# Moving two GpSimd additions of `bv` behind the block differences of `h` in a fused two-layer graph kernel

## Chip, cores and metric

The kernel runs on one core of one Trainium2 chip. The metric is the device time of one execution in microseconds; the time before is the median of three runs. All arithmetic is in float32.

## What is computed

128 batches, each a 128 x 512 matrix `x` (128 nodes, 512 features). Layer 0 adds to every row a number that depends on the adjacency matrix; layer 1 is multi-head attention with 8 heads of 64, masked where the adjacency is zero:

```python
h = relu(layernorm(x))
A = adj @ h;  C = adj @ h + b
x = x + max over n' of relu(A[o, n] + C[o, n'] - A[o, n'])
h = relu(layernorm(x))
q, k, v = h @ Wq + bq, h @ Wk + bk, h @ Wv + bv
w = softmax(q k^T / 8 + mask(adj))
x = x + w v
```

In layer 0 the two matrices are the same, so `C - A` is the bias `b` alone and the layer adds to a row a number of that row: `relu(max(adj @ h) + b)`. A number per row does not change a layernorm over the row, so one normalisation serves both layers. The weights of a softmax sum to one, so `bv` can be added to `x` directly instead of to `v`. That is what the moved additions do: `x += bv` for a batch, on GpSimd.

## The kernel before

The 128 batches are taken in 32 groups of 4 (`G`, L54; `NG`, L184). The loop over groups (L700) is a software pipeline, in an order that is written out by hand: `tc.manual_schedule()` (L655) leaves each engine the order in which the program issues its instructions. While group g goes through attention, the inputs of the projections of group g+1 are prepared, and the layernorms of group g+2 run. Here `m` (L717) is the first batch of group g+2.

**A group's stages.** First `apply(g-1)` (L584): attention weights times V, 128 TensorE matmuls at L600, and the normalisation on VectorE at L617 and L618. Then `scores(g)` (L563): 64 matmuls at L570, exponentials on ScalarE at L578. Then comes a list of steps (`part`, L705): six for the product h Wv of group g (v), six for h Wq of group g+1 (q), six for h Wk (k). Behind step s the program issues all that `todo[s]` holds (L757 to L761).

**The products.** `Products` (L392) forms each projection by a Strassen-like scheme with 7 products of half size, called p1, p6, p2, p7, p5 and the pair p4 and p3; all their matmuls have line L421 (`mm`). The last two products are in turn split once more into 128 x 128 blocks, in two parts: `p43a` (L492) directly behind p7 and `p43b` (L511) behind p5. Their matmuls have line L487 (`block_mm`). Results come out of PSUM by VectorE additions: L460 in p6, L469 in p7, L442 in p5 and p43b (`add`), and L490 (`more`), which adds a small block from the PSUM bank `scr` (L479) onto `u` in SBUF. `p43a` fills `scr` and ends with three L490 additions out of it. `p43b` first writes into the same `scr`, so its first matmuls on TensorE wait for these three. It then adds from `scr` once more (fourth L490), and its last four matmuls write into `scr` again and wait for that addition.

**The operands.** The scheme needs sums of quarters of h: `h_sum` (L340, instruction at L345), four subtractions of two SBUF tiles into `hs` on VectorE per group, for the next group. They are issued behind steps 0, 1, 2 and 2 of a group (L727), except in group 0. The blocks need differences as well: `h_blocks` (L347, instructions at L359), six subtractions on GpSimd into the single buffer `h2`, issued behind steps 5 and 6 (L729). The old `h2` is read by the matmuls of v's `p43b` until then.

**The layernorms.** `norm(m)` (L264) computes statistics on VectorE (L279 to L282) and from them `rstd` and `nmr` on GpSimd (L284, L286). `norm_end(m)` (L288) computes `hn` on ScalarE (L289) and then calls `add_bv(m)` (L293), a GpSimd addition of two SBUF tiles of 128 x 512, in place in the tile `xp` of x (L295). `blocks(m)` (L297) transposes `hn` in 32 x 32 blocks on VectorE (L302), `move` sends the blocks to their places by DMA, and `adjacency(m)` (L324) is the layer-0 product (L327) and its maximum (L328). `next_norms(m)` (L644) says behind which step each of these is issued for groups 0 to 29: `norm_end` of m and m+1 behind step 0, `norm` and `norm_end` of m+2 behind step 8 and of m+3 behind step 12.

**GpSimd's other work in a group.** Four additions of the residual for the group before (L630), and eight multiplications of the attention weights by the mask (`mask`, L580, instruction at L582) behind steps 8 to 15, which `apply` of the next group needs.

Of the kernel before, what the change touches and what calls it, by code (L numbers as in the profile page):

```python
# [53 lines left out]
G = 4  # L54
# [113 lines left out]
def tile_adj_preln_d2(  # L168
# [38 lines left out]
    def fast(ctx):  # L207
# [15 lines left out]
        def x_of(b):  # L223
            return X[b // 2][:, b % 2, :]
# [60 lines left out]
            nmr = NMR[m] = stat.tile([P, 1], F32, name="nmr")  # L285
            nc.gpsimd.tensor_scalar(nmr, mv[:, 0:1], rstd, -1.0, op0=ALU.mult, op1=ALU.mult)  # L286

        def norm_end(m):  # L288
            nc.scalar.activation(HN[m], x_of(m), AF.Relu, scale=RSTD[m], bias=NMR[m])  # L289
            if m >= G:  # L290
                add_bv(m)

        def add_bv(m):  # L293
            x_m = x_of(m)
            nc.gpsimd.tensor_tensor(x_m, x_m, bv_sb, op=ALU.add)  # L295
# [348 lines left out]
        def next_norms(m):  # L644

            return {
                0: [(norm_end, m), (norm_end, m + 1)],
                4: [(blocks, m)], 6: [(blocks, m + 1), (move, m + 1)], 7: [(adjacency, m)],
                8: [(norm, m + 2), (norm_end, m + 2)],
                12: [(norm, m + 3), (norm_end, m + 3), (adjacency, m + 1)],  # L650
                13: [(blocks, m + 2)],
                14: [(blocks, m + 3), (move, m + 3), (adjacency, m + 2)],
            }

        with tc.manual_schedule():  # L655
# [44 lines left out]
            for g in range(NG):  # L700
# [16 lines left out]
                m = b + 2 * G  # L717
                if g + 1 < NG:
# [12 lines left out]
                    if g + 2 < NG:  # L731
                        for s, l in next_norms(m).items():
                            for what in l:
                                add(s, *what)
                    else:
                        add(6, count, 0, b)
# [73 lines left out]
```

## Time and profile before

| what | value |
|---|---|
| time, median of 3 runs (lowest, highest) | 1538.81 us (1538.68, 1539.62) |
| span of the profiled execution | 1538.4 us |
| VectorE busy | 1080.2 us, 70% |
| GpSimd busy | 869.5 us, 57% |
| ScalarE busy | 507.0 us, 33% |
| granted TensorE clock, mean | 0.998 |
| GpSimd L295, the additions of bv | 128, mean 1464 ns, 186.1 us in all |
| GpSimd L582, the masks | 240, mean 1271 ns, 297.4 us in all |
| DMA | 105.32 MB, mean 68 GB/s |

PE stands for TensorE's matmuls, PEld for its weight loads, DVE for VectorE, ACT for ScalarE, POOL for GpSimd. Durations of an instruction are in ns, everything else is in us. In the timeline, a row gives the start, the time from the first start to the last end of the instructions merged in it (x8 is eight of them), the engine, the line and the operation with its tiles, and in brackets the idle time of the engine just before and what ended it. The ends of matmuls are modelled, so for TensorE the starts are the better measure.

### The profile page before, as it was taken

To read this page: it belongs to the slowest core of one execution; us is meant where nothing else is said; L and a number is where in the kernel's file an instruction comes from. 1 tells how busy PE (TensorE), PEld (TensorE's weight loads), DVE (VectorE), ACT (ScalarE), POOL (GpSimd) and SP (SyncE) were. 2 spreads that over 40 slices of the span, in tenths; PEclk is the share of its full clock that TensorE was granted. 3 is DMA by queue.
4 is the path that set the end of the run, shared out by engine and by line. 5 is a ranking of instruction groups with operands and counts; after the bars stand their busy time and mean duration, and the time that the engine had idled before them with its cause. 6 is when DMAs were issued, how large, how long until landed. Compare 5 with 4: busy or idle time off the path is not lost. (4 is left out here: it accounts for less than half of the span.)

```text
span 1538.4 us, 33066 instructions
## 1 busy us (share of the span) xinstructions
PE 1507.3 (98%) x12909; PEld 1322.5 (86%) x12909; DVE 1080.2 (70%) x2187; ACT 507.0 (33%) x970; POOL 869.5 (57%) x968
## 2 busy tenths in 40 slices
PE   8999999999999999999999999999999999999997
PEld 6888888888888888888888888888888888888886
DVE  6677677776777767677767777677676767776766
ACT  3333323333243332333332333324333233333232
POOL 5676556556565564655655655656556465565620
PEclk9999999999999999999999999999999999999999
DMA  5222222223222232222322222322223222232211
GB/s 169 52 68 79 60 62 73 64 75 78 47 73 66 72 83 43 75 65 73 79 56 65 74 64 76 72 52 73 65 72 84 42 75 68 70 80 56 51 33 57
DMA packets 307807, 105.32 MB, mean 68 GB/s; under 512 B 273153, under 2 KB 273281, under 8 KB 307649
## 3 DMA queue, kind: packets, MB, share of 16 engines
q1 hardware_dynamic: 307328, 102.84, 26.0%
q8 instruction: 104, 1.70, 0.5%
q14 instruction: 55, 0.44, 0.1%
q0 software_dynamic: 176, 0.27, 0.1%
q10 hardware_dynamic: 144, 0.07, 0.0%
HBM read 37.03 MB, written 33.55 MB: 46 GB/s over the span
## 5 line engine op out<-in xcount | busy, mean ns | idle before, releaser
L630 POOL TENSOR_TENSOR o<-xp,o 128x512 f32<-128x512 f32 x122 | 151.0, 1270 | 312.6 <-DVE o L618 269.3
L582 POOL TENSOR_TENSOR w<-w,live 128x512 f32<-128x512 f32 x240 | 297.4, 1271 | 0.0
L490 DVE TENSOR_TENSOR u<-u,bk 128x256 f32<-128x256 f32 x552 | 206.0, 415 | 120.3 <-PE bk L487 113.1
L578 ACT ACTIVATE w<-bk 128x512 f32<-128x512 f32 x256 | 128.8, 628 | 345.4 <-PE bk L570 345.4
L295 POOL TENSOR_TENSOR xp<-xp,bv_sb 128x512 f32<-128x512 f32 x128 | 186.1, 1464 | 61.0 <-ACT hn L289 61.0
L421 PEld LDWEIGHTS bk<-hs,sk_sb 128*128 128x128 f32 x768 | 143.7, 190 | 44.5 <-issue 29.2
L421 PE MATMUL bk<-hs,sk_sb 128*128 128x256 f32 x768 | 181.4, 379 | 0.0
L421 PE MATMUL bk<-sv_sb,hs 128*128 128x256 f32 x768 | 181.2, 379 | 0.0
L421 PE MATMUL bk<-hs,sq_sb 128*128 128x256 f32 x744 | 175.9, 379 | 0.0
L421 PEld LDWEIGHTS bk<-sv_sb,hs 128*128 128x128 f32 x768 | 143.8, 190 | 30.9 <-issue 14.3
L328 DVE TENSOR_REDUCE amax<-bk 128x1 f32<-128x512 f32 x128 | 88.2, 689 | 108.0 <-PE bk L327 105.1
L421 PEld LDWEIGHTS bk<-hs,sq_sb 128*128 128x128 f32 x744 | 139.1, 190 | 17.5
L284 POOL TENSOR_TENSOR rstd<-ve,mhalf 128x1 f32<-128x1 f32 x128 | 83.5, 653 | 95.1 <-DVE ve L282 94.9
L289 ACT ACTIVATE hn<-xp,nmr,rstd 128x512 f32<-128x512 f32 x124 | 100.8, 814 | 104.7 <-POOL nmr L286 104.7
L469 DVE TENSOR_TENSOR u<-bk,u 128x512 f32<-128x512 f32 x95 | 65.3, 688 | 91.8 <-PE bk L421 89.7
L327 PE MATMUL bk<-hn,adjT 128*128 128x512 f32 x248 | 126.7, 592 | 0.0
L600 PE MATMUL bk<-v,w 128*64 128x65 f32 x4096 | 126.6, 222 | 0.0
L600 PEld LDWEIGHTS bk<-v,w 128*64 128x64 f32 x4096 | 122.1, 137 | 4.1 <-issue 0.3
L421 PE MATMUL bk<-wv_sb,hT 128*128 128x256 f32 x512 | 124.3, 386 | 0.0
L570 PE MATMUL bk<-qT,kT 64*128 64x128 f32 x2048 | 122.9, 275 | 0.0
L421 PE MATMUL bk<-hT,wk_sb 128*128 128x256 f32 x512 | 121.1, 380 | 0.0
L570 PEld LDWEIGHTS bk<-qT,kT 64*128 64x128 f32 x2048 | 116.8, 188 | 2.5 <-issue 0.3
(149 smaller groups left out, 2576.6 us busy)
## 6 DMA issues: line engine op xcount, KB each, us to landing
out_dram<-o SPq DMA_DIRECT2D x128, 256.0 KB, 2.0
xp<-in_x_dram SPq DMA_DIRECT2D x62, 512.0 KB, 3.8
hT<-tb SPq DMA_DIRECT2D x992, 32.0 KB, 1.9
xp<-in_x_dram SPq DMA_DIRECT2D x4, 256.0 KB, 4.1
wq_sb<-in_L_gnn_Wq_dram SPq DMA_DIRECT2D x2, 512.0 KB, 7.7
wk_sb<-in_L_gnn_Wk_dram SPq DMA_DIRECT2D x2, 512.0 KB, 9.7
wv_sb<-in_L_gnn_Wv_dram SPq DMA_DIRECT2D x2, 512.0 KB, 10.3
bv_sb<-in_L_gnn_bv_dram POOLq DMA_DIRECT2D x1, 256.0 KB, 6.8
```

Of the source, the lines that this page charges most:

```text
L284: nc.gpsimd.tensor_tensor(rstd, ve, mhalf, op=ALU.pow)
L289: nc.scalar.activation(HN[m], x_of(m), AF.Relu, scale=RSTD[m], bias=NMR[m])
L295: nc.gpsimd.tensor_tensor(x_m, x_m, bv_sb, op=ALU.add)
L327: nc.tensor.matmul(pa, adjT, HN[m], start=True, stop=True)
L328: nc.vector.reduce_max(AMAX[g][:, i : i + 1], pa, axis=AX.X)
L421: nc.tensor.matmul(bank[:, r, :], lhs, rhs, start=first and r == 0 and c == 0, stop=r == 1 and c == 1, skip_group_check=True,)
L490: nc.vector.tensor_tensor(to, to, what, op=ALU.add)
L570: nc.tensor.matmul(psc[j][:, f, :], KT[g][r, f, i * D : (i + 1) * D], QT[g][r, f, i * D : (i + 1) * D], start=True, stop=True,)
L578: nc.scalar.activation(w[:, j], psc[j], AF.Exp, scale=HD ** -0.5)
L582: eng.tensor_tensor(w[:, j], w[:, j], live_h, op=ALU.mult)
L600: nc.tensor.matmul(pav[r, c : c + HE], w[:, h % 2, h // 2, r], V[:, i, h, :], start=True, stop=True,)
L630: eng.tensor_tensor(y, x_of(b), y, op=ALU.add)
```

## The change

`norm_end` gets an argument, by which `next_norms` leaves out the additions of bv for the first two batches of a group (m and m+1), and issues them behind step 6 instead. There they come behind both `h_blocks` calls (which the loop adds to steps 5 and 6 ahead of `next_norms`). The additions for m+2 and m+3 stay where they are, and so does every instruction of the other engines. It is for GpSimd's order: the additions no longer stand directly behind the `nmr` of m+1, and fill the place behind the block differences.

```diff
-        def norm_end(m):
+        def norm_end(m, bv=True):
             nc.scalar.activation(HN[m], x_of(m), AF.Relu, scale=RSTD[m], bias=NMR[m])
-            if m >= G:
+            if m >= G and bv:
                 add_bv(m)
@@
             return {
-                0: [(norm_end, m), (norm_end, m + 1)],
-                4: [(blocks, m)], 6: [(blocks, m + 1), (move, m + 1)], 7: [(adjacency, m)],
+                0: [(norm_end, m, False), (norm_end, m + 1, False)],
+                4: [(blocks, m)],
+                6: [(blocks, m + 1), (move, m + 1), (add_bv, m), (add_bv, m + 1)], 7: [(adjacency, m)],
                 8: [(norm, m + 2), (norm_end, m + 2)],
```

In GpSimd's queue, a group's instructions before and after:

```
before: 4 x L630, rstd, nmr, rstd, nmr, 2 x L295, 6 x L359,           rstd, nmr (m+2), L295, 5 x L582, ...
after:  4 x L630, rstd, nmr, rstd, nmr,           6 x L359, 2 x L295, rstd, nmr (m+2), L295, 5 x L582, ...
```

## The prediction

> **What bounds the kernel now.** I read the page's busy times first, then the waits, then one group in the timeline, engine by engine.
>
> ```profile
> PE 1507.3 (98%) x12909; PEld 1322.5 (86%) x12909; DVE 1080.2 (70%) x2187; ACT 507.0 (33%) x970; POOL 869.5 (57%) x968
> ```
>
> TensorE is the bound, with 31 us of the span idle, start and end included. A change on GpSimd can only pay through a wait of TensorE. The list of waits (engine, line, waited for, us in total, times, longest) has few of these:
>
> ```profile
> POOL h L359 <- PE bk L487: 155.4, 30, 9.9
> PEld bk L487 <- DVE u L490: 27.2, 29, 1.1
> PE bk L487 <- DVE u L490: 15.6, 29, 0.7
> ```
>
> TensorE never waits for GpSimd. It waits 29 times for VectorE's L490, once per group. And the block differences L359, ahead of which the additions of bv stand, wait for TensorE for 5 us in nearly every group, so a place nearer the front of GpSimd's queue gives them nothing. The question is what makes L490 late. One group (g = 10) in the timeline, rows of GpSimd, VectorE and TensorE in order of time:
>
> ```profile
> 525.99 3.38 POOL L295 TENSOR_TENSOR xp<-xp,bv_sb 128x512 f32<-128x512 f32 x2
> 526.49 1.75 DVE L345 TENSOR_TENSOR hs<-hT 128x512 f32<-128x512 f32 x1
> 528.17 1.75 DVE L345 TENSOR_TENSOR hs<-hT,hs 128x512 f32<-128x512 f32 x1
> 529.34 1.89 PE L421 MATMUL bk<-sv_sb,hs 128*128 128x256 f32 x8
> 529.85 0.68 DVE L469 TENSOR_TENSOR u<-bk,u 128x512 f32<-128x512 f32 x1
> 530.63 1.08 DVE L490 TENSOR_TENSOR u<-u,bk 128x256 f32<-128x256 f32 x3
> 531.77 0.71 PE L487 MATMUL bk<-ssv_sb,h 128*128 128x128 f32 x4 [0.53 <-DVE u L490]
> 534.10 1.89 PE L421 MATMUL bk<-hT,wq_sb 128*128 128x256 f32 x8
> 534.35 0.73 POOL L359 TENSOR_TENSOR h<-hT 128x256 f32<-128x256 f32 x1 [4.97 <-PE bk L487]
> ```
>
> The third and fourth h_sum take 1.75 us and lie under the two additions of bv. L469, the three L490 and then p43b on TensorE follow without a gap. Group 30 runs the same v product, and `next_norms` gives it no additions of bv:
>
> ```profile
> 1473.98 0.68 DVE L345 TENSOR_TENSOR hs<-hT 128x512 f32<-128x512 f32 x1
> 1474.59 0.69 DVE L345 TENSOR_TENSOR hs<-hT,hs 128x512 f32<-128x512 f32 x1
> 1476.16 0.69 DVE L469 TENSOR_TENSOR u<-bk,u 128x512 f32<-128x512 f32 x1 [0.89 <-PE bk L421]
> 1476.85 1.89 PE L421 MATMUL bk<-sv_sb,hs 128*128 128x256 f32 x8
> 1478.58 0.61 PE L487 MATMUL bk<-ssv_sb,h 128*128 128x128 f32 x4
> 1481.01 0.81 PE L421 MATMUL bk<-hT,wq_sb 128*128 128x256 f32 x3
> ```
>
> There the same two h_sums take 0.68 and 0.69 us, VectorE waits 0.89 us for TensorE instead, and p43b starts 1.73 us behind p5 (1478.58 - 1476.85) instead of 2.43 (531.77 - 529.34). This is the comparison that carries the forecast.
>
> [...] L345 (two SBUF inputs) is stretched under L295, from 0.69 to 1.75 us, and of the two L295 the pair takes 3.38 us where two undisturbed ones would take 2.5 (the masks L582 of the same shape: 1.27 us). L460, L469, L442 and L490, with one input in PSUM, have a maximum of 694 ns (L490: 423 ns) over all their executions, many of them under masks. [...]
>
> **The change part by part.**
>
> 1. *Removed from behind the nmr of m+1.* GpSimd is then idle from 526.0 (the end of the second nmr) until L359. The third and fourth h_sum fall from 1.75 to 0.69 us, so VectorE is done with them about 2.1 us earlier: in group 30 the fourth ends 1.05 us behind the start of p7 (1475.28 - 1474.23). L469 then waits for p7's matmuls, as in group 30 and as in q, where it starts 2.0 us behind p7 (542.14 - 540.14); in v of group 10 it is 3.12 (529.85 - 526.73). So L469 and the three L490 come 1.1 to 1.2 us earlier. In group 30 the L490 end at 1478.13, 0.24 us ahead of the weight load of p43b (1478.37): the wait of 0.93 us on the weight load is gone whole.
>
> 2. *What appears in its place.* In p43b the last four matmuls wait for the fourth L490. That queue on VectorE is L442 (p5), then `blocks(m)` L302 of 0.70 us from step 4, then L490. With p43b late, L490 has time; with p43b on time, it does not quite. In q, where nothing stands between L442 and L490, the stretch from p5's first matmul to the next product's first is 546.72 - 542.76 = 3.96 us. In group 30 a mask of 0.68 us stands there (L582 on VectorE at 1479.39), and the stretch is 1481.01 - 1476.85 = 4.16. So of the 4.76 us in group 10 (534.10 - 529.34), 0.80 are lost, and I take 0.60 of them to come back; with 0.70 in place of 0.68 us, 0.58. I take 0.59.
>
> 3. *How many groups.* I followed this stretch through the trace: it is 4.76 to 4.78 us in 27 of the groups 1 to 29, and 4.92 and 4.64 in the two others; 3.96 in q throughout but one at 4.07. Group 0 does not count: its h_sums come behind steps 3 to 5, when its additions (51.62 to 54.11) are over, and they take 0.68 us already. So 29 groups: 29 x 0.59 = 17.1 us.
>
> 4. *Added behind the block differences.* L359 waits for the last read of `h2` by p43b (534.35, GpSimd idle 4.97 us before), and its six take 3.56 us until 537.91. The two additions follow: their cost is between 2.5 us (2 x 1.27, undisturbed) and 3.4 (as now). What is queued behind is rstd of m+2, which waits for VectorE's statistics until 540.46. 537.91 + 2.5 = 540.4: they fit. At 3.4 rstd is 0.9 us late. Who waits for that: nmr, hn(m+2), its addition, five masks, and the last mask ends at 556.95. `apply` begins at 560.29, so 3.3 us are free: nothing reaches TensorE. The hn of m+2 on ScalarE delays the p1a of k at 548.65, ahead of which ScalarE idles 5.81 us. I take 0.
>
> 5. *VectorE under the new place.* It runs L302, L460, L328 and L279 there (536.29 to 539.90): each has one SBUF input at most. L279 keeps 677 to 695 ns in all 128 executions, though some lie under masks. I take 0. In group 0 the differences end at 63.8, so the two additions end at 66.3 to 67.2; the rstd behind them starts at 66.75 now, so it is at most 0.4 us late, ahead of the same slack: 0.
>
> 6. *No new wait.* The additions wait for hn of the same batch, done at 526.9. Nobody reads the new xp until add_c, two groups later.
>
> Sum: 1538.8 - 17.1 = 1521.7 us.
>
> **The rivals.**
>
> *The whole loss comes back* (7%). If L302 and L490 are in time for the last four matmuls: 29 x 0.80 = 23.2, so 1515.6. Against it stands group 30, whose mask is as long as L302.
>
> *Nothing happens* (5%). If the h_sums are slow for a reason of their own, such as the DMA traffic (GpSimd's additions lie in the stretch with 116 to 223 GB/s), they stay at 1.75: 1538.8. For it: in group 30, where they are short, the traffic is lower too (66 GB/s from 1472 to 1476). Against: the L345 at 524.57 lies in the densest traffic of the group (223 GB/s) and takes 0.69.
>
> *The collision moves, and it is slower* (4%). If L460, L328 and L279 were stretched by 1.06 us each under the additions, q's L469 (idle 1.76 us before) would come 3.18 - 1.76 = 1.42 late. In v, 1.12 to 1.19 late cost 0.80, so some 1.1 here: 29 x (1.1 - 0.59) = +15, 1554. Against: the fixed durations of these lines.
>
> **How the numbers follow.** My case has 84%. Its own bounds are 29 x 0.58 = 16.8 and, if part of the 0.2 returns, up to the 23.2 of the first rival; downwards, a wait like the one of L302 might cost 0.2 more: 29 x 0.4 = 11.6, 1527.2. The range is 1515 to 1527; it leaves out the last two rivals. Faster by over 0.2% (3.1 us): 91%; within: 5%; slower: 4%.
>
> **What would show it.** In the profile after: L345 near 690 ns in all groups (now 1191 and 1196 on average); L295 near 1270; the wait of L487's weight load for L490 no longer 0.93 but 0.1 to 0.2 us, in the last four matmuls; the stretch from p5 to q's p1 at 4.16 to 4.18; a group's period 0.6 us shorter. It is wrong if L345 stays long, if L460, L328 or L279 become longer, or if TensorE waits elsewhere for what these 0.6 us uncover.

## The result, and the profile after

The changed kernel takes 1521.37 us (median of 4 runs, 1520.96 to 1521.57); the kernel before takes 1538.85 us beside it. The ratio is 0.9885, with a 95% interval of 0.9868 to 0.9902: faster by 17.5 us. Forecast were 1521.7 us, in a range of 1515 to 1527.

The page's busy times and two rows of the waits (engine, line, waited for, us in total, times, longest), after the change:

```profile
PE 1504.1 (99%) x12909; PEld 1325.6 (87%) x12909; DVE 1023.2 (67%) x2187; ACT 507.3 (33%) x970; POOL 844.4 (56%) x968
POOL h L359 <- PE bk L487: 233.8, 30, 9.9
DVE u L469 <- PE bk L421: 114.6, 94, 2.7
```

VectorE lost 57 us of busy time (1080.2 before) and GpSimd 25 us (869.5), with as many instructions as before. The two waits of TensorE's L487 for L490 are gone from the list. VectorE's L469 now waits for TensorE 94 times instead of 65: in the 29 groups in question the late one has become the early one. The timeline of a group (g = 10, the one shown of before), rows of VectorE, TensorE and GpSimd in order of time:

```profile
519.97 0.68 DVE L345 TENSOR_TENSOR hs<-hT 128x512 f32<-128x512 f32 x1
520.58 0.68 DVE L345 TENSOR_TENSOR hs<-hT,hs 128x512 f32<-128x512 f32 x1
522.13 0.69 DVE L469 TENSOR_TENSOR u<-bk,u 128x512 f32<-128x512 f32 x1 [0.88 <-PE bk L421]
522.82 1.89 PE L421 MATMUL bk<-sv_sb,hs 128*128 128x256 f32 x8
523.02 1.08 DVE L490 TENSOR_TENSOR u<-u,bk 128x256 f32<-128x256 f32 x3 [0.20 <-PE bk L487]
524.55 0.61 PE L487 MATMUL bk<-ssv_sb,h 128*128 128x128 f32 x4
525.36 0.70 DVE L302 STREAM_TRANSPOSE tb<-hn 128x512 f32<-128x512 f32 x1
525.99 0.38 DVE L490 TENSOR_TENSOR u<-u,bk 128x256 f32<-128x256 f32 x1
526.11 0.39 PE L487 MATMUL bk<-sv_sb,h 128*128 128x128 f32 x2
526.42 0.71 PE L487 MATMUL bk<-ssv_sb,h 128*128 128x128 f32 x4
526.97 1.89 PE L421 MATMUL bk<-hT,wq_sb 128*128 128x256 f32 x8
527.22 0.73 POOL L359 TENSOR_TENSOR h<-hT 128x256 f32<-128x256 f32 x1 [7.71 <-PE bk L487]
530.73 2.50 POOL L295 TENSOR_TENSOR xp<-xp,bv_sb 128x512 f32<-128x512 f32 x2
533.33 0.55 POOL L284 TENSOR_TENSOR rstd<-ve,mhalf 128x1 f32<-128x1 f32 x1
```

The two h_sums take 0.68 us instead of 1.75. p43b on TensorE starts 1.73 us behind p5 (524.55 - 522.82), the stretch from p5 to q's first product is 526.97 - 522.82 = 4.15 us, and it is 4.14 or 4.15 in all of the groups 1 to 29. A group's period fell from 47.37 us (529.34 and 576.71 are p5 of groups 10 and 11 before) to 46.75 (522.82 and 569.57). The two additions take 2.50 us in their new place and end at 533.23, and rstd of m+2 starts at 533.33.

From group 1's p5 to group 30's, the trace of before has 1373.85 us (103.00 to 1476.85) and that of after 1355.85 (102.07 to 1457.92): 18.0 us, in 29 groups. The profiled spans differ by 19.2 us; most of the rest comes from ahead of the groups, where TensorE's first large products (L546) started 1.1 us earlier in the profiled execution of the changed kernel (12.15 against 13.29), before any of the changed code. The timed difference, 17.5 us, is close to that of the groups.

### The profile page after: what moved, and what is told of

The parts are those of the page before. It is cut to its first block, busy times and chain, and to the rows that moved or that the text cites. A ratio compares the mean times of both kernels' runs of the same rounds, so it can differ in the third digit from the quotient of the medians.

```text
span 1519.2 us, 33036 instructions
## 1 busy us (share of the span) xinstructions
PE 1504.1 (99%) x12909; PEld 1325.6 (87%) x12909; DVE 1023.2 (67%) x2187; ACT 507.3 (33%) x970; POOL 844.4 (56%) x968
## 4 chain that ended last, share of the span: by engine, by line
PE 99%; DVE 0%; DMA 0%; POOL 0%; ACT 0%; DVEq 0%; issue 0%
PE bk L421 55%; PE bk L487 19%; PE bk L600 8%; PE bk L570 8%; PE bk L327 7%; PE bk L546 1%; PE bk L321 0%; DMA xp<-in_x_dram 0%; DVE o L618 0%; ACT o L289 0%; DVE live L639 0%; DVE st L279 0%; DVE RS L617 0%; DVE o L630 0%; DVEq L776 0%; POOL rstd L284 0%
## 5 line engine op out<-in xcount | busy, mean ns | idle before, releaser
L490 DVE TENSOR_TENSOR u<-u,bk 128x256 f32<-128x256 f32 x552 | 205.7, 414 | 115.4 <-PE bk L487 111.3
L295 POOL TENSOR_TENSOR xp<-xp,bv_sb 128x512 f32<-128x512 f32 x128 | 161.1, 1269 | 59.5 <-ACT hn L289 58.6
L328 DVE TENSOR_REDUCE amax<-bk 128x1 f32<-128x512 f32 x128 | 88.2, 689 | 105.4 <-PE bk L327 102.5
L359 POOL TENSOR_TENSOR h<-hT 128x256 f32<-128x256 f32 x31 | 22.6, 728 | 238.2 <-PE bk L487 233.8
L421 PEld LDWEIGHTS bk<-hs,sq_sb 128*128 128x128 f32 x744 | 138.9, 190 | 17.7
L469 DVE TENSOR_TENSOR u<-bk,u 128x512 f32<-128x512 f32 x95 | 65.8, 692 | 116.7 <-PE bk L421 114.6
```

What stands on the lines that cost most here:

```text
L328: nc.vector.reduce_max(AMAX[g][:, i : i + 1], pa, axis=AX.X)
L421: nc.tensor.matmul(bank[:, r, :], lhs, rhs, start=first and r == 0 and c == 0, stop=r == 1 and c == 1, skip_group_check=True,)
L490: nc.vector.tensor_tensor(to, to, what, op=ALU.add)
```

## Experiments

My theory: a two-input h_sum on VectorE and a GpSimd instruction that reads SBUF lengthen each other (in group 10 before, the h_sum takes 1.75 us instead of 0.69, each addition 1.7 instead of 1.27); the stretched h_sums make L469 and the three L490 late, and TensorE's p43b waits for them; behind that a second, shorter wait stands, on the transpose L302. The rivals: it is the place of `x += bv` in the order that counts, not what it collides with (order); any work of GpSimd slows VectorE (busy); the loss is proportional to the number of additions (proportional); v's product is longer of itself. A further rival, that DMA traffic makes the h_sums slow, is settled by the changed kernel's own trace (see the part on the prediction). All times below are medians beside the kernel before on the same chip, 1539.6 us for the first four and 1539.5 for the last three. In the kernels e1 to e3 the lines behind L296 have numbers 5 higher.

### e1: the additions again in the old place, as dummies

In the three kernels e1 to e3, `extra` stands in the old place of the additions, whose own place remains the new one. Its output is a tile that nobody reads at that time, so this is additional work only.

```diff
+        def extra(m):
+            t = tmp.tile([P, 2, HT2], F32, name="p1a", bufs=1).rearrange("p a b -> p (a b)")
+            for i in range(2):
+                nc.gpsimd.tensor_tensor(t, x_of(m + i), bv_sb, op=ALU.add)
@@
-                0: [(norm_end, m, False), (norm_end, m + 1, False)],
+                0: [(norm_end, m, False), (norm_end, m + 1, False), (extra, m)],
```

> The changed kernel, and in the place which the two additions of bv left (behind the nmr of m+1) two additions of the same operands into a tile that nobody reads; the moved additions stay behind the block differences. Extra work, same output. Collision of reads: the third and fourth h_sum are 1.75 us again, v's stretch from p5 to the next product 4.76 us, the time that of the kernel before, 1538.8 (+-1.5). Rival 'order' (the gain is that x += bv itself comes later, and what depends on it): no effect, 1521.4.

Measured: 1539.58 us, ratio 1.0000 (0.9992 to 1.0009). Its timeline, rows of GpSimd, VectorE and TensorE:

```profile
525.30 3.39 POOL L300 TENSOR_TENSOR p1a<-xp,bv_sb 128x512 f32<-128x512 f32 x2
525.80 1.76 DVE L350 TENSOR_TENSOR hs<-hT 128x512 f32<-128x512 f32 x1
527.48 1.75 DVE L350 TENSOR_TENSOR hs<-hT,hs 128x512 f32<-128x512 f32 x1
528.65 1.89 PE L426 MATMUL bk<-sv_sb,hs 128*128 128x256 f32 x8
533.41 0.81 PE L426 MATMUL bk<-hT,wq_sb 128*128 128x256 f32 x3
```

The whole gain is gone, the h_sums take 1.76 and 1.75 us, and the stretch is 4.76 us again (528.65 to 533.41), though the additions that count stand in their new place. The rival "order" falls: what matters is what runs beside the h_sums.

### e2: GpSimd busy in the old place, reading nothing

```diff
-            for i in range(2):
-                nc.gpsimd.tensor_tensor(t, x_of(m + i), bv_sb, op=ALU.add)
+            for i in range(4):
+                nc.gpsimd.memset(t, 0.0)
```

> The changed kernel, and in the old place four GpSimd memsets of 128x512 into a tile that nobody reads: GpSimd is busy but reads nothing from SBUF. Collision of reads: h_sum stays at 0.69 us, 1521.4 (+-1.5). Rival 'busy' (any work of GpSimd beside h_sum slows it[...]): h_sums stretched as far as the memsets last, up to 1538.8.

Measured: 1521.83 us, ratio 0.9885 (0.9869 to 0.9902), as the changed kernel.

```profile
520.18 2.27 POOL L300 MEMSET p1a<- 128x512 f32 x4
520.70 0.68 DVE L350 TENSOR_TENSOR hs<-hT 128x512 f32<-128x512 f32 x1
521.31 0.68 DVE L350 TENSOR_TENSOR hs<-hT,hs 128x512 f32<-128x512 f32 x1
```

Four memsets fill 2.27 us, and the h_sums under them keep 0.68. The rival "busy" falls: beside the memsets, which only write, an h_sum takes 0.68 us, and beside the additions of e1, which also read, 1.75.

### e3: one input instead of two

```diff
-            for i in range(2):
-                nc.gpsimd.tensor_tensor(t, x_of(m + i), bv_sb, op=ALU.add)
+            for i in range(3):
+                nc.gpsimd.tensor_scalar(t, x_of(m + i % 2), 1.0, 2.0, op0=ALU.mult, op1=ALU.add)
```

> The changed kernel, and in the old place three GpSimd multiply-adds with constants, each reading one SBUF tile of 128x512, into a tile that nobody reads. Collision of reads: one read is enough, h_sums are stretched; how far depends on the length of one such instruction, estimated at 0.6 to 1.3 us from the two-input 1.27; if the h_sums are done more than 0.9 us later than in the changed kernel, TensorE waits: between 1521.4 and 1538.8, nearer to the second. Rival 'two inputs on both sides are needed': 1521.4.

Measured: 1521.40 us, ratio 0.9883 (0.9866 to 0.9899). As a time this missed the "nearer to the second" that I expected.

```profile
519.74 3.08 POOL L300 TENSOR_SCALAR p1a<-xp 128x512 f32<-128x512 f32 x3
520.23 1.09 DVE L350 TENSOR_TENSOR hs<-hT 128x512 f32<-128x512 f32 x1
521.25 1.09 DVE L350 TENSOR_TENSOR hs<-hT,hs 128x512 f32<-128x512 f32 x1
522.39 0.69 DVE L474 TENSOR_TENSOR u<-bk,u 128x512 f32<-128x512 f32 x1
523.08 1.89 PE L426 MATMUL bk<-sv_sb,hs 128*128 128x256 f32 x8
```

But the collision is there: both h_sums are stretched, from 0.68 to 1.09 us, so here one SBUF input on GpSimd is enough, and the rival that needs two on both sides falls by the trace, not by the time. The time is unchanged because the delay is 0.82 us in all, less than the 0.88 us that VectorE had idle ahead of L469 (L474 in this kernel). It starts without a wait now, but on time: 0.69 us ahead of p5, as in the changed kernel (523.08 - 522.39, and 522.82 - 522.13 there).

### e4: one of the two additions put back

```diff
-                0: [(norm_end, m, False), (norm_end, m + 1, False)],
+                0: [(norm_end, m), (norm_end, m + 1, False)],
@@
-                6: [(blocks, m + 1), (move, m + 1), (add_bv, m), (add_bv, m + 1)], 7: [(adjacency, m)],
+                6: [(blocks, m + 1), (move, m + 1), (add_bv, m + 1)], 7: [(adjacency, m)],
```

> The changed kernel with the addition of batch m back in its old place, that of m+1 behind the block differences. Slack: one addition stretches at most one or two h_sums, by about 1.06 us in all. In the changed kernel VectorE waits 0.88 us for TensorE ahead of L469 and the three L490 end 0.24 us ahead of their use, together 1.1 us, so hardly anything is lost: 1521.4 to 1523. Rival 'proportional': half the gain lost, 1530.

Measured: 1520.93 us, ratio 0.9878 (0.9862 to 0.9895). Nothing is lost; the stretch is 4.15 us.

```profile
520.67 1.76 DVE L345 TENSOR_TENSOR hs<-hT 128x512 f32<-128x512 f32 x1
522.35 0.68 DVE L345 TENSOR_TENSOR hs<-hT,hs 128x512 f32<-128x512 f32 x1
522.95 0.68 DVE L469 TENSOR_TENSOR u<-bk,u 128x512 f32<-128x512 f32 x1
523.52 1.89 PE L421 MATMUL bk<-sv_sb,hs 128*128 128x256 f32 x8
523.73 1.08 DVE L490 TENSOR_TENSOR u<-u,bk 128x256 f32<-128x256 f32 x3
```

One h_sum is stretched by the one addition. That costs VectorE 1.07 us. 0.88 us of idle time ahead of L469 take most of it: L469 starts 0.57 us ahead of p5 instead of 0.69. What is left goes into a second idle time, which the expectation did not count: in the changed kernel VectorE waits 0.20 us more, for TensorE's blocks, between L469 and the three L490. That wait is gone here, and the L490 start 0.21 us behind p5, against 0.20. The 0.24 us by which they end early are hardly touched. "Proportional" (1530) falls: the slack is 0.88 + 0.20 + 0.24 = 1.3 us, one collision of 1.07 us fits into it and two (2.1 us) do not.

### e5: the other partner moved instead

```diff
-                    for k, s in enumerate((0, 1, 2, 2) if g > 0 else (3, 3, 4, 5)):
+                    for k, s in enumerate((0, 1, 5, 5) if g > 0 else (3, 3, 4, 5)):
```

This is the kernel before, with both additions in the old place.

> The kernel before with the other partner moved: the additions of bv stay behind the nmr of m+1, and the third and fourth h_sum are issued behind step 5 instead of 2 (group 0 as before). Collision of reads: L295 back at 1.27 us, L469 in time, v's stretch 4.15; but the h_sums now lie beside the block differences L359, which read two SBUF tiles too, and ahead of L460 of q: both may be stretched, by up to about 2 us of the 0.83 and 1.76 idle there. 1521 to 1525. Rival 'order' (the additions' place alone decides): 1538.8.

Measured: 1522.64 us, ratio 0.9891 (0.9875 to 0.9908).

```profile
530.30 0.68 DVE L345 TENSOR_TENSOR hs<-hT 128x512 f32<-128x512 f32 x1
531.66 0.73 POOL L359 TENSOR_TENSOR h<-hs 128x256 f32<-128x256 f32 x1 [1.50 <-DVE hs L345]
```

The stretch in v is 4.14 or 4.15 in all 29 groups: the gain is had without touching the additions. The collision with the block differences that I feared hardly takes place, because the fourth difference waits for the fourth h_sum, and GpSimd is idle meanwhile. The time is 1.3 us above that of the changed kernel, or 0.9 us by the two ratios to the kernel before. From group 1's p5 to group 30's the two traces are equally long (1355.88 and 1355.85 us). Behind that e5 has a wait, once, in group 30, where VectorE has the checks of `count` (L639, L640) behind the h_sums and reaches q's L460 late. In the list of waits:

```profile
PEld bk L421 <- DVE u L460: 1.2, 1, 1.2
PE bk L421 <- DVE u L460: 0.8, 1, 0.8
```

The 0.8 us of the matmuls fit the difference of the ratios, though that difference is within their intervals.

### e6 and e7: the second wait

e6 is the changed kernel, e7 the kernel before, each with one edit: the transpose of the first batch is issued behind step 5, and so behind the fourth L490.

```diff
-                4: [(blocks, m)],
+                5: [(blocks, m)],
```

> The changed kernel with blocks(m) (the transpose L302) behind step 5 instead of 4, so that it stands behind the fourth L490 of v's p43b on VectorE. If the 0.2 us that v's stretch keeps over q's (4.15 against 3.96) are L302's, the stretch is 3.96 in groups 1 to 29, and the time 29 x 0.19 = 5.5 us less than that of the changed kernel: 1515.9 (+-1), a ratio to the kernel before of 0.985. Rival: v's product is longer of itself, 1521.4; or the later transpose delays L460 (0.83 us idle before it) and gives it back.

Measured: 1515.97 us, ratio 0.9849 (0.9832 to 0.9865), 5.4 us less than the changed kernel (from group 1's p5 to group 30's, 1350.44 us against 1355.85). TensorE and VectorE in e6 from p5 to q's p6:

```profile
521.40 1.89 PE L421 MATMUL bk<-sv_sb,hs 128*128 128x256 f32 x8
523.94 0.41 DVE L490 TENSOR_TENSOR u<-u,bk 128x256 f32<-128x256 f32 x1
524.69 0.39 PE L487 MATMUL bk<-sv_sb,h 128*128 128x128 f32 x2
524.91 0.61 PE L487 MATMUL bk<-ssv_sb,h 128*128 128x128 f32 x4
525.36 0.81 PE L421 MATMUL bk<-hT,wq_sb 128*128 128x256 f32 x3
529.09 0.69 DVE L460 TENSOR_TENSOR u<-bk,p1a 128x512 f32<-128x512 f32 x1 [0.24 <-PE bk L421]
```

L490 is done at 524.35, well ahead of 524.91, and the stretch is 3.96 us as in q (from p5 at 521.40 to 525.36), in every group from 1 to 29 within 0.01. The transpose now takes 0.6 us of the idle time ahead of L460 and leaves 0.24. This version is the fastest of all; its period is 46.56 us.

> The kernel before with blocks(m) behind step 5 instead of 4, the additions of bv where they were. While p43b starts 0.7 us late, the fourth L490 is in time anyway (stretch 4.76 = 3.96 + 0.80, all from the three L490): no effect, 1538.8 to 1539.6. Rival 'the two losses add': 29 x 0.2 = 5.5 us faster.

Measured: 1539.55 us, ratio 1.0001 (0.9992 to 1.0010).

```profile
532.47 0.42 DVE L490 TENSOR_TENSOR u<-u,bk 128x256 f32<-128x256 f32 x1 [0.20 <-PE bk L487]
```

Alone the same edit gives nothing. L490 waits for TensorE here, which the first wait has already made late. So the two waits do not add: the first hides the second, and the second comes out when the first is removed.

## Why the prediction was right

*The bound* (TensorE, which waits in a group only for L490): right. Both waits left the list, and TensorE's busy share rose to 99%. That TensorE never waits for GpSimd holds for the groups; the list has one such wait, of 4.8 us, at the start of the program (L260), before and after.

*Step 1* (the h_sums fall to 0.69 us, and the wait ahead of p43b goes whole): right in size. On average L345 fell from 1191 and 1196 ns to 703 and 716; the long ones left, three of 1.64 to 1.75 us, are in the start of the program, where they lie beside GpSimd's sums of weights (L384, 1.55 to 1.72 us). L469's idle time of 0.88 us and the 1.73 us to p43b are those of group 30 before (0.89 and 1.73), which had served as the model. That the reads of GpSimd are the cause was not shown when the forecast was made; e1 and e2 show it: with reads in the old place the h_sums take 1.75 us and the loss is back (1539.58 us), with writes alone they take 0.68 and it is not (1521.83). The rival in which DMA traffic makes the h_sums slow falls too: in the changed kernel the third and fourth take 0.68 us under 240 GB/s (519.97 to 521.26). The forecast's argument against it was weaker than it says: the undisturbed h_sum at 524.57 lay under 303 GB/s by the trace (the forecast has 223), and the densest traffic, 360 GB/s from 526 to 527, came only with the start of the slow third one. But the trace of before could have settled it: the fourth, just as slow, ran from 528.17 to 529.92, where the DMA moved 0 GB/s.

*Step 2* (about 0.20 of the 0.80 us stay, for L302): right. 4.15 us was measured, 0.19 above q's 3.96, where group 30 has 4.16 and I took 4.17. e6 shows that it is L302 and not the product. The rival in which the whole loss comes back (1515.6) needed this one edit more, and then came to 1515.97.

*Step 3* (29 groups): right; 29 x (4.76 - 4.15) = 17.7 us, against a measured 17.5.

*Steps 4 and 5* (the new place costs nothing): right. The pair takes 2.50 us, the lower end, and ends 0.1 us ahead of rstd's start. L295 has a maximum of 1288 ns over all 128. L460, L328 and L279, which lie beside it (at 530.70, 531.48 and 532.09 in group 10), keep a maximum of 692, 693 and 694 ns: the rival in which the collision moves falls with that.

The one expectation of the list that did not show as written: the wait on the last four matmuls, 0.1 to 0.2 us, is no entry of the list of waits. It is seen in the starts alone, 0.31 us between the last two groups of L487 in the changed kernel (526.11 of the pair ahead of it to 526.42) against 0.22 (524.69 to 524.91) in e6. That is 0.09 us; the other 0.10 lie between the last group and q's first product (526.42 to 526.97 against 524.91 to 525.36).

## What to carry to other kernels

When an elementwise instruction shows two durations, look at what the other elementwise engine reads at that moment. Here a VectorE instruction with two SBUF inputs and a GpSimd instruction that reads SBUF cost each other time: beside additions with two inputs the h_sum took 1.75 us instead of 0.68 and an addition 1.7 instead of 1.27; beside e3's instructions with one input it took 1.09, and three of these took 3.08 us together. The profile shows the lost time as busy, not as waiting (VectorE's busy time was 1080.2 us before and 1023.2 after). The cure here was to move either of the two: the additions to where VectorE runs L460 (one input in PSUM, one in SBUF), L328 (one in PSUM) and L279 (one in SBUF), which kept at most 694 ns there (1521.37 us), or the h_sums to where GpSimd is idle, 1.50 us ahead of the fourth difference (e5, 1522.64 us). The worth was not the sum of the stretches but what exceeded the slack behind them: without both collisions, of 1.07 us each, the way from p5 to q's first product became 0.61 us shorter (4.76 to 4.15), and with e6's edit as well 0.80 (3.96); one collision alone cost nothing (e4, 4.15). A group that by chance lacks one of the partners is a model of the change, measured in the trace of before, with the wait that will come out next.

## What I had not expected of the hardware

The stretch of an h_sum differs with the length of the GpSimd instruction beside it: with additions of 1.27 us it is 1.76 - 0.69 = 1.07, with the one-input instructions of e3, of 0.62 us where undisturbed (the shortest was 613 ns), it is 1.09 - 0.69 = 0.40. In both cases that is the length of the GpSimd instruction less 0.2 us. In e4, where only one addition is there, only one h_sum is stretched (1.76 us, the next 0.68). My estimate from these four durations (1.27 and 1.76, 0.62 and 1.09) is that an h_sum is held up by one GpSimd instruction at a time, for most of its length; no run tests it further.
